# Turning softmax weights by 32x32 blocks on VectorE and moving the blocks by transfers, in a gated cross-attention and mixture kernel

## The chip, the cores and the metric

The kernel runs on one core of one Trainium2 chip. The metric is the time of one execution on the device, in microseconds (us). Before the change the median of three runs is 1311.29 us (1310.93 to 1311.45).

## The reference

There are 8 batches; x and the context are (8, 512, 2048) in float32. The last axis is cut into patches of 128 columns, and each patch attends within itself with 8 heads of 32 rows. Cut to what matters:

```python
def xattn(qk, v, masks, Wq, bq, Wk, bk, Wv, bv, Wo, bo):   # per patch of W = 128 columns
    q   = einsum('ed,bdw->bew', Wq, qp) + bq[:, None]       # 256 x 128
    k   = einsum('ed,bdw->bew', Wk, qp) + bk[:, None]
    val = einsum('ed,bdw->bew', Wv, vp) + bv[:, None]
    scores = einsum('bhdi,bhdj->bhij', qh, kh) / sqrt(32)
    scores = where(mp[:, :, None, :] > 0, scores, -1e9)
    attn = softmax(scores, axis=-1)
    o = gelu(einsum('bhij,bhdj->bhdi', attn, vh), approximate=False)
    return (einsum('de,bew->bdw', Wo, o) + bo[:, None]) * masks

x = x + tanh(g_xattn) * xattn(layernorm(x), ctx, mask, ...)
x = x + tanh(g_ffn) * ffn(layernorm(x), ...)   # router over 64 experts, the 8 best weights,
                                               # flat * their sum + weights @ expert_bias
```

## The kernel before

The columns of all batches are cut into 32 chunks of 512 (four per batch), and each chunk into two pairs of patches. The main loop (L816) handles one pair per turn, g from 0 to 61; such a turn is called a slot here. An even slot takes the first pair of chunk ch = g // 2, an odd one the second. Pairs 62 and 63 are handled by a written-out tail from L1025 on. The order of the work is written out by hand: every engine executes its instructions in the order in which the code issues them, and waits at an instruction until its operands are there.

A slot does, in TensorE's order: the scores of pair g (L412, 32 matmuls into four PSUM banks sc0 to sc3); the weighing of pair g - 2 (weigh, L487, tile pa); in even slots two row blocks of the output product of chunk ch - 2 (attend, L524, tile po), in odd slots the router's logits of chunk ch - 2 (L557, tile pl); then the queries and keys of the next chunk, in half of their rows (L343), by a seven-product scheme: seven blocks of two matmuls in four PSUM banks (tile qk). After that come the values of the next chunk (L391, tile pv), in even slots the turning of x (turn_x, L549, tile px), in odd slots two more blocks of the output product, and the mixture of experts of an older chunk (mixed, L695, tile pb).

The softmax of pair g: VectorE forms maxima over the keys from the scores and writes the negated scores to SBUF (maxima, L431, 16 instructions, 128x128 each); ScalarE takes the exponentials with their sums (exps, L446, 16 instructions); VectorE inverts the sums and POOL multiplies (divide, L458, once for each of the two patches). The weights then lie with the query on the partition, and the weighing needs the key there. They are turned one slot later, in pair g - 1's four steps of four TensorE transposes (turn, L468, tile pt), each copied out of PSUM by ScalarE (turned, L482, tile atT). In an even slot, two steps stand before the queries and keys, one among the values and one after turn_x; in an odd slot one before, two within (by the function between, L915) and one after the queries and keys.

Keys are multiplied by 1/sqrt(32) where the mask is on and by 0 where it is off (mask, L296, and L387). The same tile becomes an additive bias afterwards (mask_bias, L301) and is added in maxima. The eviction of the values adds bv on VectorE (L406). Gelu follows the weighing (L520), on ScalarE.

Buffers: the products qk, po, pl and pb share two PSUM buffers in turn (tag mm, function product at L311), except where a caller names one of the score banks: in the steady slots pv takes sc0, and an odd slot's two po take sc1 and sc2. Transposes and pa share two others (tag tr). A buffer's next product waits until the engine that reads the last one is done. The weights at have four buffers of one patch each.

SP issues nearly all DMAs, in program order: context (L102), normalized input (L96), x for the residual (L113), pieces of x for the statistics (L91, after the bn_stats of the piece before in that buffer), masks (L107) and the store (L711). The transfers use eight completion semaphores in turn.

In every eight slots, one batch of the mixture is prepared: an aggregate of statistics (fin 2), the choice of experts (fin 3, gather_halves, add_halves and choose), and the selection of the 8 best (fin 4, select and turn_weights, tile pw).

Of the kernel before, what the change touches and what calls it, by code (L numbers as in the profile page):

```python
# [15 lines left out]
P = 128  # L16
EPS = 1e-5
NEG = -1e9
# [4 lines left out]
def flamingo_gated_kernel(  # L23
# [43 lines left out]
    SW = 512  # L67
    scale = 1.0 / math.sqrt(DH)
# [54 lines left out]
    bv_sb = const.tile([P, DK], F32, name="bv_sb")  # L123
# [30 lines left out]
    def load_rest():  # L154
# [3 lines left out]
        nc.sync.dma_start(bv_sb, bv.partition_broadcast(P))  # L158
        with nc.allow_non_contiguous_dma(reason="short bias vectors onto partitions"):
            nc.sync.dma_start(bq_sb, bq.rearrange("(t p) -> p t", p=P))  # L160
            nc.sync.dma_start(bk_sb, bk.rearrange("(t p) -> p t", p=P))
            nc.sync.dma_start(bo_sb, bo.rearrange("(t p) -> p t", p=P))
        nc.sync.dma_start(gates[:, 0:1], g_xattn.partition_broadcast(P))
# [130 lines left out]
    qss, kss, vTs, m01s = {}, {}, {}, {}  # L294

    def mask(ch):  # L296

        m01s[ch] = work.tile([P, CW], F32, tag="m01", name=f"m01_{ch}")
        nc.vector.tensor_scalar(m01s[ch], mks[ch], 0.0, scale, ALU.is_gt, ALU.mult)

    def mask_bias(ch):  # L301

        nc.vector.tensor_scalar(m01s[ch], m01s[ch], 0.0, NEG, ALU.is_equal, ALU.mult)

# [15 lines left out]
    def first_queries_and_keys():  # L320
# [4 lines left out]
        for m in range(NM):  # L325
            for i, (w, e, pt) in enumerate(parts):
# [10 lines left out]
                else:  # L337
                    nc.vector.scalar_tensor_tensor(
                        kss[0][:, e, :], pt, bk_sb[:, e : e + 1], m01s[0], ALU.add, ALU.mult
# [3 lines left out]
    def queries_and_keys(ch, e, between):  # L343
# [6 lines left out]
        s1, s5, u2, u4 = (  # L350
            work.tile([P, CW // 2], F32, tag=t, name=f"{t}_{ch}_{e}", bufs=1)
            for t in ("s1", "s5", "u2", "u4")
        )
# [25 lines left out]
        u3 = work.tile([P, CW // 2], F32, tag="s1", name=f"u3_{ch}_{e}", bufs=1)  # L379
# [7 lines left out]
        nc.vector.tensor_tensor(k, k, m01s[ch], ALU.mult)  # L387
# [14 lines left out]
    def values_out(ch, h):  # L402
# [3 lines left out]
        nc.vector.tensor_tensor(vT, pv, bv_sb[:, None, :].to_broadcast([P, NPP, DK]), ALU.add)  # L406
# [5 lines left out]
    def scores(g):  # L412
# [14 lines left out]
        at = [work.tile([P, H, W], F32, tag="at", name=f"at_{g}_{i}", bufs=4) for i in range(NPP)]  # L427
# [3 lines left out]
    def maxima(g, qs):  # L431
# [4 lines left out]
        for q in qs:  # L436
            i = q // 2
            bias = m01s[ch][:, hf * HW + i * W : hf * HW + (i + 1) * W]
            for r in (2 * (q % 2), 2 * (q % 2) + 1):
                for e in range(NE):  # L440
                    nc.vector.tensor_tensor_reduce(  # L441
                        p["at"][i][:, e * HR + r, :], p["sc"][r][:, i, e, :], bias, -1.0, BIG,
# [25 lines left out]
    def turn(g, k):  # L468
# [3 lines left out]
        if e == 0:  # L472
            p["atT"][i] = work.tile([P, H, W], F32, tag="atT", name=f"atT_{g}_{i}")
# [5 lines left out]
    def copy(engine, out_, in_):  # L479
        (engine.tensor_copy if engine is nc.vector else engine.copy)(out_, in_)  # L480

    def turned(g, k, engine=nc.scalar):  # L482
        p = pairs[g]
        i, e = k // NE, k % NE
        copy(engine, p["atT"][i][:, e * HR : (e + 1) * HR, :], p.pop("pt"))

    def weigh(g):  # L487
# [7 lines left out]
        for i in range(NPP):  # L495
            for h in range(H):
                e, r = h // HR, h % HR
                nc.tensor.matmul(  # L498
                    pa[r * DH : (r + 1) * DH, e, i, :], vTs[ch, hf][:, i, h * DH : (h + 1) * DH],
                    p["atT"][i][:, h, :], start=True, stop=True,  # L500
# [19 lines left out]
    def gelu(ch, cs=whole):  # L520
        o = os_[ch][:, :, cs]
        nc.scalar.activation(o, o, AF.Gelu)  # L522
# [143 lines left out]
    def turn_weights(b, mps=range(NM // 2)):  # L666
        t = experts[b]
        rest, s = t["rest"], span(mps)
        if 0 in mps:

            pool, tag = (work, "s1") if late else (small, "wT")
# [98 lines left out]
    for m in range(NM):  # L770
# [6 lines left out]
        if m == NM - 1:  # L777
            mask(0)
            weight_sums()
            values_out(0, 0)  # L780
            values_out(0, 1)
            values_out(1, 0)
        next(projections)
    mask_bias(0)
# [31 lines left out]
    for g in range(NG - NH):  # L816
# [5 lines left out]
        g2 = g - 2 if g >= 2 else None  # L822
# [14 lines left out]

        def turn_(k):
            if g1 is not None:
                turn(g1, k)  # L840
                turned(g1, k)
# [18 lines left out]
        if g2 is not None:  # L860
            weigh(g2)
            weighed(g2)
# [11 lines left out]
        exps(g, 0)  # L874
        if even:
# [4 lines left out]
            exps(g, 1)  # L880
            exps(g, 2)
            if g > 0:
                mask(nxt)
            read_x(len(over), over)
            turn_(0)
            turn_(1)
            exps(g, 3)
            if fin != 4:
                for k in steps:
                    scale_x(mb, k)  # L890
            if g > 0:
                divide(g, 0)
            if g == 0:
                load_mask(2)
        else:
            exps(g, 1)
            if lch is not None:
                logits(lch)
                logits_out(lch)
            if g > 1:  # L900
                read_x(len(over), over)
            turn_(0)
            exps(g, 2)
            exps(g, 3)
            for k in steps:
                scale_x(mb, k)
            if g > 1:
                divide(g, 0)
# [5 lines left out]

        def between(i):  # L915
            if even:
                if g == 0 and i == 0:
                    divide(g, 0)
                    mask(nxt)
                turn_x_(i)  # L920
            elif i == 0:
                if g == 1:
                    divide(g, 0)
                turn_(1)
                if fin == 3:
                    gather_halves(b4)
                if pch is not None:
                    gelu(pch)
            else:
                if g == 1:  # L930
                    read_x(len(over), over)
                turn_(2)
                if pch is not None and nxt < last:
                    load_mask(nxt + 1)

# [3 lines left out]
        if not even:  # L939
            mask_bias(nxt)  # L940
# [3 lines left out]
        divide(g, 1)  # L944
        if not even and nxt < last:
# [3 lines left out]
            sums_of_x(nxt + 1, 0)  # L949
# [278 lines left out]
```

## Time and profile before

| what | value |
|---|---|
| median of 3 runs | 1311.29 us |
| span of the profiled execution, first to last instruction | 1309.1 us |
| busy: POOL | 796.3 us (61%) |
| granted TensorE clock, mean | 0.999 of full speed |
| an even slot (598.53 to 618.34) | 19.81 us: TensorE 19.81, VectorE 14.44, ScalarE 12.80, POOL 16.27 |
| an odd slot (618.34 to 638.22) | 19.88 us: TensorE 19.88, VectorE 12.92, ScalarE 13.63, POOL 7.86 |
| eight slots (378.91 to 538.31) | 159.40 us: TensorE 159.40, VectorE 114.22, ScalarE 108.08, POOL 100.18 |
| DMA | 173.40 MB, mean 132 GB/s; the SP queue 40.0% of 16 engines' span |

PE is TensorE's matmul, PEld its weight load, DVE VectorE, ACT ScalarE, SPq the issuing queue of SP. Busy times are of one profiled execution. Lines such as "L462 POOL ... xN | busy, mean | idle <- releaser" name a line of the kernel, the engine, the output and input tiles with buffer numbers left out, how many instructions there are, their busy time in us, the mean of one in ns, and how long the engine stood idle before them and for whom. In a timeline the columns are start and duration in us; the durations of neighbours overlap a little, so costs are taken from one start to the next. A matmul of float32 counts as two instructions.

### The profile page before, as it was taken

To read this page: it belongs to the slowest core of one execution; us is meant where nothing else is said; L and a number is where in the kernel's file an instruction comes from. 1 tells how busy PE (TensorE), PEld (TensorE's weight loads), DVE (VectorE), ACT (ScalarE), POOL (GpSimd) and SP (SyncE) were. 2 spreads that over 40 slices of the span, in tenths; PEclk is the share of its full clock that TensorE was granted. 3 is DMA by queue.
4 is the path that set the end of the run, shared out by engine and by line. 5 is a ranking of instruction groups with operands and counts; after the bars stand their busy time and mean duration, and the time that the engine had idled before them with its cause. 6 is when DMAs were issued, how large, how long until landed. Compare 5 with 4: busy or idle time off the path is not lost.

```text
span 1309.1 us, 27778 instructions
## 1 busy us (share of the span) xinstructions
PE 1292.1 (99%) x9532; PEld 941.1 (72%) x9532; DVE 923.7 (71%) x3605; ACT 872.2 (67%) x2843; POOL 796.3 (61%) x817
## 2 busy tenths in 40 slices
PE   8999999999999999999999999999999999999997
PEld 5777777777777777777777777777777777777653
DVE  5777676777677767777677776677776776666776
ACT  2776776676675766766676766677756767657654
POOL 3655456765566755566655666656666665566645
PEclk9999999999999999999999999999999999999999
DMA  8444324344345353444443453533543423423124
GB/s 273 111 126 122 112 78 137 106 161 127 116 153 162 123 167 97 136 165 142 140 148 95 154 169 124 159 108 123 165 151 132 159 63 127 138 97 106 69 78 177
DMA packets 109725, 173.40 MB, mean 132 GB/s; under 512 B 9232, under 2 KB 43664, under 8 KB 109456
## 3 DMA queue, kind: packets, MB, share of 16 engines
q1 hardware_dynamic: 107264, 168.75, 40.0%
q10 hardware_dynamic: 2320, 2.88, 0.6%
q8 instruction: 75, 1.23, 0.4%
q14 instruction: 66, 0.54, 0.1%
HBM read 138.06 MB, written 33.55 MB: 131 GB/s over the span
## 4 chain that ended last, share of the span: by engine, by line
PE 91%; ACT 3%; DVE 3%; DMA 1%; POOL 1%; issue 0%; DVEq 0%; ACTq 0%
PE qk L360 27%; PE po L528 17%; PE pv L397 15%; PE pt L476 8%; PE sc L422 5%; PE pa L498 5%; PE pb L702 5%; PE pl L563 4%; PE px L552 4%; ACT at L453 2%; DMA xr<-in_x 1%; DVE st L547 1%; DVE st L249 1%; PE pf L327 1%; ACT atT L480 0%
## 5 line engine op out<-in xcount | busy, mean ns | idle before, releaser
L462 POOL TENSOR_TENSOR at<-at,rsum 128x1024 f32<-128x1024 f32 x128 | 244.2, 1908 | 291.1 <-DVE rsum L461 269.2
L453 ACT ACTIVATE at<-at,nmx 128x128 f32<-128x128 f32 x1024 | 396.4, 392 | 3.2 <-DVE nmx L441 3.2
L397 PE MATMUL pv<-wv_sb,cx 128*128 128x256 f32 x1024 | 237.8, 380 | 1.7 <-DMA cx<-in_ctx 1.6
L528 PE MATMUL po<-o,wo_sb 128*128 128x512 f32 x512 | 234.1, 599 | 0.4 <-ACT o L522 0.4
L441 DVE CUSTOM_DVE_ANT_0 at<-sc,m 128x128 f32<-128x128 f32 x1024 | 220.7, 286 | 7.6 <-PE sc L422 7.4
L397 PEld LDWEIGHTS pv<-wv_sb,cx 128*128 128x128 f32 x1024 | 187.5, 191 | 24.8 <-DMA cx<-in_ctx 3.2
L537 POOL TENSOR_TENSOR xr<-t,xr 128x512 f32<-128x512 f32 x124 | 161.4, 1313 | 65.8 <-DVE t L534 65.7
L453 ACT ACTIVATION_READ_ACCUMULATOR at<-at,nmx 128x1 f32 x1024 | 194.9, 190 | 0.0
L480 ACT COPY o<-pa 128x512 f32<-128x512 f32 x63 | 36.9, 585 | 230.3 <-PE pa L498 230.3
L480 ACT COPY atT<-pt 128x512 f32<-128x512 f32 x254 | 140.5, 576 | 52.9 <-PE pt L476 52.7
L528 PEld LDWEIGHTS po<-o,wo_sb 128*128 128x128 f32 x512 | 94.3, 190 | 100.6 <-issue 83.9
L476 PEld LDWEIGHTS pt<-ident,at 128*128 128x128 f32 x1024 | 121.8, 141 | 57.2 <-issue 35.5
L476 PE MATMUL pt<-ident,at 128*128 128x128 f32 x1024 | 150.7, 275 | 1.3 <-ACT atT L480 0.9
L534 DVE SCALAR_TENSOR_TENSOR t<-po,bo_sb,mk 128x512 f32<-128x512 f32 x128 | 95.7, 749 | 62.5 <-PE po L528 62.2
L480 ACT COPY x1T<-px 128x512 f32<-128x512 f32 x120 | 70.2, 585 | 96.8 <-PE px L552 96.6
L360 PE MATMUL qk<-xt,wq_sb 128*128 128x256 f32 x496 | 128.0, 380 | 1.6 <-DVE u L368 1.6
L360 PE MATMUL qk<-xn,wk_sb 128*128 128x256 f32 x496 | 127.5, 380 | 0.0
L360 PE MATMUL qk<-xn,ws 128*128 128x256 f32 x496 | 127.3, 379 | 0.0
L360 PEld LDWEIGHTS qk<-xn,ws 128*128 128x128 f32 x496 | 94.2, 190 | 12.8
L720 DVE TENSOR_TENSOR xr<-pb,xr 128x512 f32<-128x512 f32 x122 | 78.2, 685 | 29.4 <-PE pb L702 29.4
L360 PEld LDWEIGHTS qk<-xn,wk_sb 128*128 128x128 f32 x496 | 89.4, 190 | 9.7
L422 PEld LDWEIGHTS sc<-ks,qs 32*128 32x128 f32 x2048 | 63.2, 186 | 45.3 <-DVE t L534 18.2
(123 smaller groups left out, 2077.7 us busy)
## 6 DMA issues: line engine op xcount, KB each, us to landing
out_dram<-xr SPq DMA_DIRECT2D x63, 512.0 KB, 3.5
cx<-in_ctx SPq DMA_DIRECT2D x61, 512.0 KB, 5.3
raw<-in_x SPq DMA_DIRECT2D x112, 256.0 KB, 3.4
xn<-in_x SPq DMA_DIRECT2D x28, 1024.0 KB, 7.8
xr<-in_x SPq DMA_DIRECT2D x28, 1024.0 KB, 7.6
mk<-in_mask_Bx1x_ff SPq DMA_DIRECT2D x32, 256.0 KB, 5.1
xr<-in_x SPq DMA_DIRECT2D x12, 256.0 KB, 6.9
cx<-in_ctx ACTq DMA_DIRECT2D x2, 512.0 KB, 8.2
```

The costliest lines, as they stand in the source:

```text
L360: nc.tensor.matmul(out_, w_[:, j, es], xb[:, j, :], start=(j == 0), stop=(j == NM // 2 - 1))
L397: nc.tensor.matmul(pv[:, i, :], cx[:, m, i * W : (i + 1) * W], wv_sb[:, m, :], start=(m == 0), stop=(m == NM - 1),)
L422: nc.tensor.matmul(sc[r][:, i, e, :], qss[ch][rows[r], e, ws], kss[ch][rows[r], e, ws], start=True, stop=True,)
L441: nc.vector.tensor_tensor_reduce(p["at"][i][:, e * HR + r, :], p["sc"][r][:, i, e, :], bias, -1.0, BIG, ALU.add, ALU.min, p["nmx"][:, r, i ...
L453: nc.scalar.activation(at, at, AF.Exp, bias=p["nmx"][:, r, i, e : e + 1], scale=-1.0, accum_out=p["rsum"][:, i, h : h + 1],)
L462: (engine or nc.gpsimd).tensor_tensor(p["at"][i], p["at"][i], rs[:, :, None].to_broadcast([P, H, W]), ALU.mult)
L476: nc.tensor.transpose(pt[:, r, :], p["at"][i][:, e * HR + r, :], ident)
L480: (engine.tensor_copy if engine is nc.vector else engine.copy)(out_, in_)
L528: nc.tensor.matmul(po[:, cs], wo_sb[:, e, m * P : (m + 1) * P], os_[ch][:, e, cs], start=(e == 0), stop=(e == NE - 1),)
L534: nc.vector.scalar_tensor_tensor(t[:, cs], po[:, cs], bo_sb[:, m : m + 1], mks[ch][:, cs], ALU.add, ALU.mult)
L537: (engine or nc.gpsimd).tensor_tensor(xc, t[:, cs], xc, ALU.add)
L720: nc.vector.tensor_tensor(xc, pt, xc, ALU.add)
```

## The change

1. In the slots, TensorE's turning (turn, turned) and its ScalarE copies are gone. VectorE turns each patch's weights in 32x32 squares, one instruction of 128x1024 per patch (turn_blocks), and then SP moves the squares between partitions with 16 transfers for a pair, each 32 partitions by 2 KB, from SBUF to SBUF (move_blocks). The tail still turns pairs 62 and 63 on TensorE.
2. Pair g - 1 is weighed in slot g (before: g - 2), and within the queries and keys, after the second PSUM bank. Its moving operand is read as four runs of 32 elements.
3. The keys aren't multiplied by the mask. The bias is made from the mask at once (NEG is -1e30), the maxima take the scale -1/sqrt(32), and mask_bias is gone.
4. The values are evicted by a plain copy on ScalarE; bv is added as the bias of gelu, which is split into its two row blocks.
5. Scratch tiles s1, u2, u3 and u4 of the queries and keys now lie in the result tiles themselves. The weights at have two buffers, blocks and atT one each.
6. Order: all exps stand before the bn_stats of leftover pieces and divide(g, 0); divide(g, 1) moves into the queries and keys; scale_x follows the moves; the sums of x are made together; norm stands ahead of the values' eviction.

```diff
-        m01s[ch] = work.tile([P, CW], F32, tag="m01", name=f"m01_{ch}")
-        nc.vector.tensor_scalar(m01s[ch], mks[ch], 0.0, scale, ALU.is_gt, ALU.mult)
-    def mask_bias(ch):
-        nc.vector.tensor_scalar(m01s[ch], m01s[ch], 0.0, NEG, ALU.is_equal, ALU.mult)
+        biases[ch] = work.tile([P, CW], F32, tag="bias", name=f"bias_{ch}")
+        nc.vector.tensor_scalar(biases[ch], mks[ch], 0.0, NEG, ALU.is_le, ALU.mult)
...
-        s1, s5, u2, u4 = (
-            work.tile([P, CW // 2], F32, tag=t, name=f"{t}_{ch}_{e}", bufs=1)
-            for t in ("s1", "s5", "u2", "u4")
-        )
+        s5 = work.tile([P, CW // 2], F32, tag="s5", name=f"s5_{ch}_{e}", bufs=1)
+        s1, u2, u3, u4 = k[:, c1], q[:, c2], q[:, c1], k[:, c2]
...
-        nc.vector.tensor_tensor(k, k, m01s[ch], ALU.mult)
...
-        nc.vector.tensor_tensor(vT, pv, bv_sb[:, None, :].to_broadcast([P, NPP, DK]), ALU.add)
+        copy(engine, vT, pv)
...
+    def turn_blocks(g, i):
+        p = pairs[g]
+        if i == 0:
+            p["blocks"] = work.tile([P, W // Q, NPP, H, Q], F32, tag="blocks", name=f"blocks_{g}", bufs=1)
+        nc.vector.transpose(
+            p["blocks"][:, :, i, :, :].rearrange("p b h j -> p h b j"),
+            p["at"][i].rearrange("p h (b j) -> p h b j", j=Q),
+        )
+    def move_blocks(g):
+        p = pairs[g]
+        t = p.pop("blocks")
+        w = work.tile([P, W // Q, NPP, H, Q], F32, tag="atT", name=f"atT_{g}", bufs=1)
+        for a in range(W // Q):
+            for b in range(W // Q):
+                nc.sync.dma_start(
+                    w[b * Q : (b + 1) * Q, a, :, :, :], t[a * Q : (a + 1) * Q, b, :, :, :]
+                )
+        for i in range(NPP):
+            p["atT"][i] = w[:, :, i, :, :].rearrange("p a h q -> p h a q")
...
-                    pa[r * DH : (r + 1) * DH, e, i, :], vTs[ch, hf][:, i, h * DH : (h + 1) * DH],
-                    p["atT"][i][:, h, :], start=True, stop=True,
+                    pa[r * DH : (r + 1) * DH, e, i, :].rearrange("p (a q) -> p a q", q=Q),
+                    vTs[ch, hf][:, i, h * DH : (h + 1) * DH],
+                    p["atT"][i][:, h, :, :], start=True, stop=True,
...
-        nc.scalar.activation(o, o, AF.Gelu)
+        for e in range(NE):
+            o = os_[ch][:, e, cs]
+            nc.scalar.activation(o, o, AF.Gelu, bias=bv_sb[:, e : e + 1])
...
         scores(g)
-        if g2 is not None:
-            weigh(g2)
-            weighed(g2)
         maxima(g, (0, 1))
...
         def between(i):
-            if even:
-                if g == 0 and i == 0:
-                    divide(g, 0)
-                    mask(nxt)
-                turn_x_(i)
-            elif i == 0:
-                if g == 1:
-                    divide(g, 0)
-                turn_(1)
+            if i == 0:
+                if g1 is not None:
+                    weigh(g1)
+                    weighed(g1)
+                if g == 0:
+                    mask(nxt)
+                divide(g, 1)
                 if fin == 3:
                     gather_halves(b4)
                 if pch is not None:
                     gelu(pch)
+                    table_of_exps()
             else:
+                turn_x_(0)
...
-                turn_(2)
                 if pch is not None and nxt < last:
                     load_mask(nxt + 1)
+                turn_blocks(g, 0)
...
         queries_and_keys(nxt, h, between)
-        if not even:
-            mask_bias(nxt)
+        turn_blocks(g, 1)
+        move_blocks(g)
+        if fin != 4:
+            for k in steps:
+                scale_x(mb, k)
```

## The prediction

> **What bounds the kernel now.** I read the engine totals first, then the chain that ended last, then the costliest groups, and last the timeline of two neighbouring slots, TensorE first and then VectorE.
>
> ```profile
> PE 1292.1 (99%) x9532; PEld 941.1 (72%) x9532; DVE 923.7 (71%) x3605; ACT 872.2 (67%) x2843; POOL 796.3 (61%) x817
> ...
> PE 91%; ACT 3%; DVE 3%; DMA 1%; POOL 1%; issue 0%; DVEq 0%; ACTq 0%
> PE qk L360 27%; PE po L528 17%; PE pv L397 15%; PE pt L476 8%; PE sc L422 5%; PE pa L498 5%; PE pb L702 5%; PE pl L563 4%; PE px L552 4%; ACT at L453 2%; DMA xr<-in_x 1%; DVE st L547 1%; DVE st L249 1%; PE pf L327 1%; ACT atT L480 0%
> ```
>
> TensorE is busy for 99% and makes 91% of the chain. The turning of the weights (pt, L476) is 8% of it, about 105 us. No other engine is over 71%. Groups:
>
> ```profile
> L462 POOL TENSOR_TENSOR at<-at,rsum 128x1024 f32<-128x1024 f32 x128 | 244.2, 1908 | 291.1 <-DVE rsum L461 269.2
> ...
> L441 DVE CUSTOM_DVE_ANT_0 at<-sc,m 128x128 f32<-128x128 f32 x1024 | 220.7, 286 | 7.6 <-PE sc L422 7.4
> ...
> cx<-in_ctx SPq DMA_DIRECT2D x61, 512.0 KB, 5.3
> raw<-in_x SPq DMA_DIRECT2D x112, 256.0 KB, 3.4
> xn<-in_x SPq DMA_DIRECT2D x28, 1024.0 KB, 7.8
> ```
>
> The timeline of TensorE in an even slot (scores at 598.53) shows where the turns stand; columns are start, duration, engine, line:
>
> ```profile
> 604.18 1.04 PE L476 MATMUL pt<-ident,at 128*128 128x128 f32 x8
> 605.06 1.03 PE L360 MATMUL qk<-xn,wk_sb 128*128 128x256 f32 x4
> ...
> 614.15 0.60 PE L476 MATMUL pt<-ident,at 128*128 128x128 f32 x4
> 614.58 1.89 PE L397 MATMUL pv<-wv_sb,cx 128*128 128x256 f32 x8
> ...
> 616.75 0.60 PE L476 MATMUL pt<-ident,at 128*128 128x128 f32 x4
> 617.28 1.13 PE L702 MATMUL pb<-eb_sb,wT 64*128 64x512 f32 x4
> 618.34 0.93 PE L422 MATMUL sc<-ks,qs 32*128 32x128 f32 x21
> ```
>
> From one start to the next, the turns take 0.88 + 0.43 + 0.53 = 1.84 us of the even slot's 19.81. In the odd slot (618.34 to 638.22, 19.88 us) the four gaps at 622.32, 626.27, 628.43 and 629.74 give 0.49 + 0.44 + 0.44 + 0.43 = 1.80. VectorE at the same places:
>
> ```profile
> 619.64 0.28 DVE L441 CUSTOM_DVE_ANT_0 at<-sc,m 128x128 f32<-128x128 f32 x1
> ...
> 623.02 0.69 DVE L581 TENSOR_TENSOR lgT<-pl,lgT 128x512 f32<-128x512 f32 x1
> ...
> 642.89 0.75 DVE L534 SCALAR_TENSOR_TENSOR t<-po,bo_sb,mk 128x512 f32<-128x512 f32 x1
> 644.07 0.75 DVE L534 SCALAR_TENSOR_TENSOR t<-po,bo_sb,mk 128x512 f32<-128x512 f32 x1 [0.43 <-PE po L528]
> ```
>
> In both slots VectorE is with the maxima until 4.67 us after the scores start (642.89 - 638.22; 623.02 - 618.34), and only then empties the first product. Today TensorE does pa and pt meanwhile.
>
> **Part 1, TensorE loses the turns.** 62 of 64 pairs lose four turns. An even slot becomes 19.81 - 1.84 = 17.97 us, an odd one 19.88 - 1.80 = 18.08.
>
> **Part 2, what is late next.** pa moves from behind the scores to behind two bank pairs of the query product. So nothing stands between po (or pl) and that product, which uses the same two PSUM buffers in turn. Even slot: po is through at 1.10 + 3.54 = 4.64 us after the scores start, but the first bank waits until t of m=2 has emptied its buffer: 4.67 + 0.67 (604.38 to the next VectorE start at 605.05) + 0.07 for the signal = 5.41. TensorE stands 0.77. Odd slot: the second bank is wanted at 1.10 + 1.87 + 1.73 = 4.70 and waits for lgT: 4.68 + 0.69 + 0.07 = 5.44, so 0.74. Slots become 18.74 and 18.82, a pair of slots 37.56 against 39.69: 2.13 saved, not 3.64.
>
> **Part 3, VectorE.** It loses the key mask product (L387, 0.60 us start to start), the values' eviction (L406, 0.60) and in odd slots L303 (0.43). It gains two block transposes of 128x1024 per slot. No row shows one. Bounds: L303 does 512 elements of one source in 0.34 start to start, so twice that less its fixed part is about 0.61; POOL's pass over the same tile is 1.91. Nearest is bn_stats, one source, 512 elements in 0.60 (2.34 us for four at L547): 1024 at that slope, 0.53 more, is 1.13, which I take.
> Even slot in order: third bank pair through at 11.61 (5.41 + 1.73 + 1.73 + 1.01 + 1.73), u and ks until 12.61, transpose to 13.74, qs to 14.08, transpose to 15.21, four bn_stats to 17.55, two to 18.75. Then the adds of pb, which TensorE releases at 18.84. VectorE is just in time: cover 0.1 us. Each 0.1 us more per transpose costs 0.2 in each of 31 even slots, 6 us in all. Odd slots have over 1 us free (transposes end at 13.5, t is due at 16.2).
> The first transpose waits for POOL's divide. In even slots POOL has two xr adds (2.6) from 5.41, so the divides end at 9.9 and 12.6, before 12.61 and 14.08. qs now overwrites u in place and waits for POOL's L381, 13.3: also before it is due. Behind a waiting transpose would stand qs, bn_stats and the next maxima.
>
> **Part 4, the moves.** 16 transfers per pair, 32 partitions x 2 KB (64 KB), all on SP, which now issues 992 more. In the changed kernel's instruction order the transfers use eight completion semaphores in turn, and each waits for the one eight before it, so the ninth move waits for the first to land. An issue takes 0.38 to 0.46 us in the SP rows; I take 0.42. Landing of 64 KB has no row: from 256 KB (3.4) and 1 MB (7.6) a straight line gives 2.35; bounds are 0, and 5.3 as for 512 KB, which is what eight in flight carry. Even slot: 15.21 + 15 x 0.42 + 2.35 = 23.9, that is 5.1 in the odd slot, where pa is due at 5.44 + 1.73 = 7.17. Room 2.0 us. From odd to even it is 13.5 to a due time of 18.82 + 8.88, room 5. Hidden, then.
> SP's queue behind them: raw (2), the store, cx, then the 1 MB xn. The odd slot's moves leave SP at 20.2, so xn is issued at about 22.0, lands 7.8 later at 11 in the even slot; norm on ScalarE starts at 14.2. Covered by 3 us.
> Here a page speaks against the change: the Trainium skill, "DMA: Bandwidth & Descriptors", Rules for kernel authors, says to coalesce small transfers, since under 64 KB mostly overhead is paid, and its bandwidth table has 64 KB at 0.95 us. Run one after another, 16 would take 15.2 us by that, past the due time by some 5 us each odd slot, an estimate of +150 us. The rows decide otherwise here, because SP need not wait for one before it issues the next.
>
> **Part 5, pa's operand.** It reads four runs of 32 elements in place of 128 in a row. No row shows such a moving operand; from 0 to a doubling of its 1.01 us per slot. I take 0: L360's matmuls take 380 ns each whether their operand is a slice of xn or all of a row of xt.
>
> **Part 6, edits at nothing.** The eviction of values goes to ScalarE behind norm: done by 17.9, due at the next scores (18.74); cover 0.8, and uncovered it would cost up to its own 0.58 per slot. The copies of atT leave ScalarE (140 us). Gelu in two halves is 0.2 us more, while pv runs on TensorE. The bias is one pass as the mask was.
>
> **The sum.** Slots 8 to 61 are 27 pairs: -57.5. Slots 4 to 7 have no pb: about -5. In each of 7 batches, select (2.65 us) stands between the transposes and pw (+0.8) and the aggregate (0.62) falls in the full even slot (+0.5): +9. Slots 0 to 3 are 10 to 18 us long, and there pa waits for moves that land 8.7 us after the transposes: +6. The two last pairs still turn on TensorE; slot 62 loses pair 61's turns: -1.5. Total -49. The profiled span of 1309.1 becomes 1260; the median of 1311.29 is 2.2 over that span, so 1262.
>
> **Rivals.**
> (a) The moves come late: slower. If a move lands in 5.3 us like cx, the ninth is issued at 5.3, the sixteenth at 8.2, and the last lands 13.5 after the transposes, 2.8 past the 10.7 us there are. 31 odd slots: +87, 1349. It decides from a landing of 3.9 us (2 x 3.9 + 7 x 0.42 = 10.7). For: it lies between the rows of 256 KB and 512 KB, and only 32 partitions are at each end. Against: 64 KB is a quarter of the smaller one.
> (b) The transpose costs 1.91: VectorE bounds the even slots, 2 x 0.78 x 31 = +48, 1310: no change.
> (c) pa doubles: 62 x 1.01 = +63, 1325. Against: nothing else in the trace slows with a slice.
> (d) The waits of part 2 don't come, since t and lgT could fall earlier: 58 slots x 0.75 = -44, 1218. Against: 4.67 is measured in both slots.
>
> **Chances.** Forecast 0.50 (1240 to 1285), (d) 0.10, (b) 0.12, (a) 0.21, (c) 0.07. Faster by over 0.2%, about what a measurement here can tell from no change: 0.50 + 0.10 + half of (b) + 0.04 of (a) = 0.70. Within: 0.03 of (b) and 0.01 of (a) = 0.04. Slower: 0.16 + 0.07 + 0.03 = 0.26. The range takes in (d), (b), (c) and the milder half of (a): 1215 to 1335.
>
> **What would show it.** In the profile after: PE pt down to some 32 transposes; a wait of the query product for t and lgT of about 0.75 us per slot; transposes near 1.13; pa with hardly a wait for DMA. Wrong if pa waits long for atT (rival a), if maxima start over 1.5 us after the scores' start (rival b), or if pa lasts over 1.1 us (rival c).

## The result, and the profile after

| | median | spread | ratio to before, 95% interval |
|---|---|---|---|
| before | 1311.36 us | 1310.93 to 1311.45 | |
| after | 1389.72 us | 1381.01 to 1392.31 | 1.0586 [1.0554, 1.0617] |

The change makes the kernel 78 us slower. The forecast was 1262 us, in a range from 1215 to 1335. The profiled execution of after took 1388.15 us, its span is 1386.3 us, and the mean granted TensorE clock in it is 0.970 of full speed (before 0.999).

The page of after, engine totals, the granted clock over the span, the main queue and the chain:

```profile
PE 1249.2 (90%) x8540; PEld 853.9 (62%) x8540; DVE 995.4 (72%) x3574; ACT 794.4 (57%) x2688; POOL 791.8 (57%) x817
...
PEclk9879999999999999999999999999999999999999
...
q1 hardware_dynamic: 155008, 233.70, 56.6%
...
PE 31%; DVE 25%; DMA 19%; SPq 11%; issue 5%; ACT 4%; POOL 4%; DVEq 0%; POOLq 0%; ACTq 0%
PE qk L355 11%; SPq L503 10%; DVE at L441 9%; DMA xn<-in_x 7%; PE po L552 7%; PE pv L390 5%; DMA out_dram<-xr 3%; DMA xr<-in_x 3%; DVE blocks L491 3%; PE pa L520 3%; DVE t L558 2%; DMA atT<-blocks 2%; PE sc L418 2%; DVE lg L650 2%; PE pb L7
```

TensorE lost 992 of its 9532 matmuls (16 transposes in each of 62 pairs), as was meant. But its busy time fell by 43 us only, while the span grew by 77 us: it is busy for 90% now, it stands for 31% of the chain in place of 91%, and most of the rest is VectorE, transfers and SP's issuing (SPq, L503: the moves). The clock row has an 8 and a 7 near the start, where before has nines.

What TensorE waited for in after (total, times, longest):

```profile
PE pa L520 <- DMA atT<-blocks: 39.5, 18, 10.6
PE sc L418 <- ACT vT L396: 38.6, 25, 7.5
PE qk L355 <- DVE t L558: 16.1, 24, 1.1
...
PE qk L355 <- DVE lgT L605: 7.2, 18, 0.7
PE qk L355 <- DVE lgT L603: 4.0, 8, 0.5
```

The last three are the waits that part 2 of the forecast worked out. The first two were not in its sum: the weighing waits for the moved weights, and the scores wait for the values, which ScalarE evicts late. SP's timeline in after (start, duration, line) shows why:

```profile
608.59 10.01 SPq L503 DMA_DIRECT2D atT<-blocks  x16
618.70 1.02 SPq L92 DMA_DIRECT2D raw<-in_x  x2
...
620.82 1.45 SPq L97 DMA_DIRECT2D xn<-in_x  x1
...
632.74 10.03 SPq L503 DMA_DIRECT2D atT<-blocks  x16
```

Sixteen moves take SP 10.0 us of issuing, 0.63 us each. That is not time spent waiting for the move eight before: among all that SP waited for ahead of its 992 moves, the landings of earlier transfers have 6.3 us in all, one of them a move's, and nearly all the rest is VectorE's turn:

```profile
SPq L503 <- DVE blocks L491: 319.5, 61, 10.8
...
SPq L503 <- DMA atT<-blocks: 0.6, 1, 0.6
```

Everything behind them on the queue starts when the sixteenth is out: raw at 618.70 and xn at 620.82 here. The landing is not the trouble; the page's rows have 64 KB moves landing in the time that the forecast took (2.35), and xn later than before (9.0 against 7.8):

```profile
atT<-blocks SPq DMA_DIRECT2D x992, 64.0 KB, 2.0
...
xn<-in_x SPq DMA_DIRECT2D x28, 1024.0 KB, 9.0
```

To place the loss, I measured each slot in the trace from its first scores to the next slot's. The four columns on the right are means in us over slots 12 to 60, by the slot's number modulo eight (3 chooses the experts, 4 selects them).

| run | median, us | slots 0-7 | slots 8-61 | even slots (0, 2 of 8) | odd slots (1, 7 of 8) | slot 3 of 8 | slot 4 of 8 |
|---|---|---|---|---|---|---|---|
| before | 1311.4 | 130.8 | 1069.5 | 19.81 | 19.88 | 20.31 | 20.03 |
| after | 1389.7 | 173.2 | 1101.1 | 19.96 | 19.94 | 22.38 | 21.47 |
| one transfer (e1) | 1309.4 | 134.4 | 1065.3 | 19.26 | 19.16 | 21.71 | 21.25 |
| one transfer, sums late (e9) | 1291.9 | 133.8 | 1045.9 | 19.26 | 19.16 | 19.73 | 20.44 |
| one transfer, sums late, t early (e14) | 1250.2 | 133.2 | 1006.3 | 18.26 | 18.37 | 18.78 | 19.53 |
| all turned on TensorE (e3) | 1409.6 | 140.5 | 1159.0 | 22.09 | 20.91 | 21.30 | 22.34 |
| mended, all late (e13) | 1274.7 | 139.2 | 1015.1 | 18.56 | 18.51 | 19.45 | 19.35 |

Of after's loss, 42 us lie in the first eight slots and 32 in the 54 that follow. The columns leave out slots 5 and 6 of eight. Slot 5 is like the other odd ones; slot 6 is longer than the slots 0 and 2: 20.75 us in after, 19.93 in e1 and e9 and 20.30 in e14, where before has 19.81. The largest single wait is in slot 1 (TensorE's timeline, the bracket is idle time and what ended it):

```profile
45.64 1.03 PE L355 MATMUL qk<-xn,ws 128*128 128x256 f32 x4
57.30 1.94 PE L520 MATMUL pa<-atT,vT 128*32 128x128 f32 x32 [10.63 <-DMA atT<-blocks]
59.16 2.08 PE L355 MATMUL qk<-xt,wq_sb 128*128 128x256 f32 x4
...
61.94 1.03 PE L355 MATMUL qk<-xt,wq_sb 128*128 128x256 f32 x4
```

The moves of pair 0 are issued from 45.56 on for 10.09 us, in a slot that took 13.5 us before. After 10.63 us of idling the same 32 matmuls of pa take 1.94 us in place of 1.08, and qk 2.08 in place of 1.03: the clock is at half. The windows say so too (length, busy time of PE, PEld, DVE, ACT, POOL, granted clock, DMA share, GB/s):

```profile
57.30:61.00 3.70, 3.70 (x36) 2.99 (x37) 0.00 (x0) 0.58 (x1) 0.00 (x0) 0.50 0.38 130
```

### The profile page after: what moved, and what is told of

It is laid out like the page before. It is cut to its first block, busy times and chain, and to the rows that moved or that the text cites. A ratio compares the mean times of both kernels' runs of the same rounds, so it can differ in the third digit from the quotient of the medians.

```text
span 1386.3 us, 27197 instructions
## 1 busy us (share of the span) xinstructions
PE 1249.2 (90%) x8540; PEld 853.9 (62%) x8540; DVE 995.4 (72%) x3574; ACT 794.4 (57%) x2688; POOL 791.8 (57%) x817
## 4 chain that ended last, share of the span: by engine, by line
PE 31%; DVE 25%; DMA 19%; SPq 11%; issue 5%; ACT 4%; POOL 4%; DVEq 0%; POOLq 0%; ACTq 0%
PE qk L355 11%; SPq L503 10%; DVE at L441 9%; DMA xn<-in_x 7%; PE po L552 7%; PE pv L390 5%; DMA out_dram<-xr 3%; DMA xr<-in_x 3%; DVE blocks L491 3%; PE pa L520 3%; DVE t L558 2%; DMA atT<-blocks 2%; PE sc L418 2%; DVE lg L650 2%; PE pb L726 2%
## 5 line engine op out<-in xcount | busy, mean ns | idle before, releaser
L441 DVE CUSTOM_DVE_ANT_0 at<-sc,bias 128x128 f32<-128x128 f32 x1024 | 220.9, 286 | 29.2 <-PE sc L418 29.2
L552 PE MATMUL po<-o,wo_sb 128*128 128x512 f32 x512 | 241.2, 614 | 0.0
L355 PE MATMUL qk<-xn,wk_sb 128*128 128x256 f32 x496 | 136.3, 397 | 27.3 <-DVE t L558 16.1
L491 DVE STREAM_TRANSPOSE blocks<-at 128x1024 f32<-128x1024 f32 x124 | 152.7, 1231 | 0.0
L355 PE MATMUL qk<-xt,wq_sb 128*128 128x256 f32 x496 | 138.5, 403 | 7.6 <-DVE qs L363 7.6
L374 DVE SCALAR_TENSOR_TENSOR qs<-qk,bq_sb,qs 128x256 f32<-128x256 f32 x62 | 30.0, 483 | 158.9 <-PE qk L355 158.9
L418 PEld LDWEIGHTS sc<-ks,qs 32*128 32x128 f32 x2048 | 70.4, 194 | 88.9 <-ACT vT L396 59.0
L418 PE MATMUL sc<-ks,qs 32*128 32x128 f32 x2048 | 85.8, 293 | 40.7 <-ACT vT L396 38.6
L520 PE MATMUL pa<-atT,vT 128*32 128x128 f32 x2048 | 72.6, 284 | 43.2 <-DMA atT<-blocks 39.5
L355 PEld LDWEIGHTS qk<-xt,wq_sb 128*128 128x128 f32 x496 | 90.4, 197 | 28.7 <-DVE qs L363 7.8
```

The costliest lines, as they stand in the source:

```text
L355: nc.tensor.matmul(out_, w_[:, j, es], xb[:, j, :], start=(j == 0), stop=(j == NM // 2 - 1))
L418: nc.tensor.matmul(sc[r][:, i, e, :], qss[ch][rows[r], e, ws], kss[ch][rows[r], e, ws], start=True, stop=True,)
L441: nc.vector.tensor_tensor_reduce(p["at"][i][:, e * HR + r, :], p["sc"][r][:, i, e, :], bias, -scale, BIG, ALU.add, ALU.min, p["nmx"][:, r, ...
L491: nc.vector.transpose(p["blocks"][:, :, i, :, :].rearrange("p b h j -> p h b j"), p["at"][i].rearrange("p h (b j) -> p h b j", j=Q),)
L520: nc.tensor.matmul(pa[r * DH : (r + 1) * DH, e, i, :].rearrange("p (a q) -> p a q", q=Q), vTs[ch, hf][:, i, h * DH : (h + 1) * DH], p["atT ...
L552: nc.tensor.matmul(po[:, cs], wo_sb[:, e, m * P : (m + 1) * P], os_[ch][:, e, cs], start=(e == 0), stop=(e == NE - 1),)
```

## The experiments

The experiments are numbered e1 to e15, and those that answer one question stand together. My theory after the traces: the loss is the issuing of the moves on SP (10.0 us per pair), which makes the weighing late and pushes xn behind it; a smaller part is the choice of experts, which now runs beside GpSimd's sums; and waits of a few us also cost TensorE its clock. The rivals: the moved bytes themselves, the block turns on VectorE, or the change's other edits.

### e1, e2 and e15: the same bytes in one transfer, in four, and in sixteen

```diff
-        for a in range(W // Q):
-            for b in range(W // Q):
-                nc.sync.dma_start(w[b * Q : (b + 1) * Q, a, :, :, :], t[a * Q : (a + 1) * Q, b, :, :, :])
+        nc.sync.dma_start(w, t)
```

e2 has four transfers, of t[rows] to w[rows] for the four groups of 32 partitions. e15 keeps all sixteen, and only their target changes: w[a * Q : (a + 1) * Q, b, :, :, :].

> The 16 moves of a pair become one transfer of the same 1 MB, written back to its own partitions, so the blocks aren't moved between partitions and the output is not the reference's; everything else stays. Theory (SP's issue pace: 16 issues at 0.63 us are 10.0 us per pair, pa and xn wait for their end): one issue of about 0.6 us is left, pa's wait on the moved blocks (39.5 us of the span on TensorE) and ScalarE's on xn (34.9 us) go, and the time falls to 1285 to 1325 us. Rival (bytes: the 65 MB more on the queue and their landing slow every other load): stays at 1370 us or above. Rival (transposes and the other edits cost it): 1350 us or above with the waits on the blocks gone.

> The 16 moves become four transfers of 256 KB, each within its own 32 partitions, so the blocks aren't moved between partitions and the output is not the reference's. Theory (cost per issue): four issues take about 2.5 us instead of 10.0, near the single transfer's time, 1290 to 1335 us. Rival (cost by bytes): as with one transfer and with sixteen, 1370 us or above. If a transfer's issue costs in proportion to its size, four take as long as sixteen and nothing is gained.

> The 16 moves stay sixteen transfers of 64 KB, but each goes from 32 partitions to the same 32 partitions, so the blocks aren't moved between partitions and the output is not the reference's. Theory (the cost is SP's issuing of sixteen transfers): as after, 1375 to 1395 us, with 10 us of issuing per pair. Rival (the crossing between partitions is what costs, and the single transfer was quick because it left that out): 1335 us or below.

Measured: 1309.44 us with one, ratio 0.9985 [0.9976, 0.9994]; 1322.60 us with four, 1.0085 [1.0070, 1.0100]. With sixteen in place it is 1388.63 us, 1.0597 [1.0577, 1.0618], the time of after. The bytes are innocent: 238 MB are moved in all of these kernels. So is the crossing of partitions, which e15 leaves out. The 80 us are gone with 15 of the 16 issues. Issuing from a second queue, which would have told SP's time apart from the number of transfers, was not run; the 10.0 us of SP against landings of 2.0 us speak for SP. With one and with four, TensorE's wait for the moved weights falls from 39.5 to 5.1 and 9.5 us, and ScalarE's for xn from 34.9 to nothing and 4.7. Four issues took 3.27 us, not 2.5: one is 0.82 us for 256 KB, 0.63 for 64 KB, and 0.47 for 1 MB over all 128 partitions, so neither their number nor their size alone sets it.

Where the issues strike can be read from TensorE's waits in slots 8 to 61, of after and then of e1:

```profile
PE sc L418 <- ACT vT L396: 30.2, 22, 2.1
...
PE pa L520 <- DMA atT<-blocks: 12.8, 13, 1.8
```

```profile
PE sc L418 <- ACT vT L396: 13.7, 9, 1.9
```

In e1 the wait for the moves is absent there. So of the 36 us between the two in these slots, 12.8 are the moves and 16.5 the values, which are evicted behind norm, which waits for xn (in e5, where xn comes early, this wait is 13.8 us, as in e1). In slots 0 to 7, 20.1 of 39 us are the moves (25.2 against 5.1).

But 1309 is not 1262 either: with the moves all but free the change is worth 2 us. Slots 3 and 4 of every eight are still long, slot 6 is no shorter than before, and the others have lost 0.55 and 0.72 us instead of 1.07.

### e3 and e10: all weights turned on TensorE again

```diff
-        turn_blocks(g, 1)
-        move_blocks(g)
+        turn_here(0, 1)
...
                 values_out(c_, h_)
+            turn_here(2, 3)
```

In e10, weigh(g1) and weighed(g1) also stand right behind scores(g).

> The change's other edits stay (mask product gone, values' evictions on ScalarE, sums of x together, pairs weighed a slot sooner), but the weights are turned on TensorE in each slot as before, with no block turns on VectorE and no moves. Theory (the moves carry most of the loss, the sums beside the choice of experts some 2 us in each of 13 slots): 1315 to 1345 us. Rival (the side edits are harmless and the moves carry all): 1305 to 1315 us. Rival (the loss lies in the side edits): 1360 us or above.

> As the kernel that turns all weights on TensorE (1409.6 us), but the pair before is weighed right behind the scores, where the product's 1.0 us stands in front of the po or pl product, instead of between queries and keys. Theory (the moved product exposed TensorE's wait for t of 0.75 us and for lgT of 0.53 us, and broke the row of query products, about 0.1 us at each break): 1.0 us less in even and 0.7 us less in odd slots, 27 pairs, 1355 to 1370 us. Rival (where the product stands doesn't matter, turning in the same slot costs it all): 1400 us or above.

Measured: 1409.63 us, 1.0748 [1.0732, 1.0764], and 1350.33 us, 1.0299 [1.0284, 1.0314]. I had expected e3 between 1315 and 1345; it came where the rival that put the loss in the side edits had it (1360 or above), and that miss was the most useful one. e10 came out 5 us below its range. Without any moves the kernel is slower than after itself. Taken against e1, it says that turning on VectorE is worth 100 us when the moves cost nothing (the forecast's part 1 has 62 pairs by 1.82, 113 us), though e3's turns stand in other places than before's. And it says that the rest of the change, with the turning put into the pair's own slot, costs 98 us against before. e10 shows where 59 of these are: in the place of pa. Behind the scores pa fills the time in which TensorE waits for t or lgT; between the banks it leaves that wait open and breaks the row of query products. This is e1's timeline in an even slot whose scores start at 639.94:

```profile
645.49 1.13 PE L355 MATMUL qk<-xn,wk_sb 128*128 128x256 f32 x4 [0.75 <-DVE t L554]
646.46 1.03 PE L355 MATMUL qk<-xt,ws 128*128 128x256 f32 x4
647.32 1.03 PE L355 MATMUL qk<-xn,wk_sb 128*128 128x256 f32 x4
648.18 1.03 PE L355 MATMUL qk<-xn,ws 128*128 128x256 f32 x4
649.14 1.08 PE L516 MATMUL pa<-atT,vT 128*32 128x128 f32 x32
650.15 1.13 PE L355 MATMUL qk<-xt,wq_sb 128*128 128x256 f32 x4
651.12 1.03 PE L355 MATMUL qk<-xn,ws 128*128 128x256 f32 x4
```

The wait is nearly the forecast's: 0.75 us of idle time by the profile, but 0.91 from start to start, as the forecast counted its 0.77 (645.49 - 641.04, less 3.54 for po); the first product stands 5.55 after the scores against 5.41. What was missing are the breaks: from start to start a row of four products takes 0.86 to 0.87 us within the run, and 0.96 or 0.97 behind the wait, ahead of pa and behind pa. The other 39 us of e10 lie in the even slots (20.84 against 19.81 in before, some 28 us) and in the first eight (139.7 against 130.8); their cause is open.

### e4 to e8: one wait at a time

e4 puts the weighing behind all queries and keys:

```diff
-                if g1 is not None:
-                    weigh(g1)
-                    weighed(g1)
...
         queries_and_keys(nxt, h, between)
+        if g1 is not None:
+            weigh(g1)
+            weighed(g1)
```

> The product of the moved weights and their evictions stand behind all queries and keys of the even slot instead of between them, some 4 us later; nothing else changes. Theory: TensorE's wait for the last move (39.5 us in all, 1 to 2 us per pair and more in the first slots) is covered by the second half of queries and keys; xn is still late behind the moves, so part of it is given back: 1350 to 1378 us. Rival (xn behind the moves sets the pace of the even slot, the wait at pa only takes its place): 1383 to 1393 us.

Measured: 1346.12 us, 1.0268 [1.0251, 1.0285], 44 us less than after and a little better than the theory's range. The wait for the moves falls from 39.5 to 3.8 us; the one of the scores for vT is still 23.9. The edit moves the weighing, and ScalarE's eviction of it, in odd slots as in even ones. Slots 8 to 61 come to 1066.7 us, which is e1's 1065.3: there the later weighing wins back all that the issues cost. What is left of it lies in slots 0 to 7 (164.7 against 134.4).

e5 issues xn ahead of the moves:

```diff
-            if nxt < last and nxt + 1 >= NCH:
-                load_xn(nxt + 1)
...
         queries_and_keys(nxt, h, between)
+        if not even and nxt + 1 < last and nxt + 2 >= NCH:
+            load_xn(nxt + 2)
```

> xn of the pair after next is issued in the odd slot ahead of the 16 moves instead of in the even slot behind them; nothing else changes. Theory: ScalarE's wait on xn (34.9 us in all) goes, norm, the values' evictions and the scores come sooner in the even slots, while pa still waits for the moves, which are now issued up to 1.5 us later: 1365 to 1383 us. Rival (pa's wait alone sets the pace): 1385 to 1400 us.

Measured: 1375.81 us, 1.0491 [1.0475, 1.0507]. ScalarE's wait for xn is gone, the even slots come to e1's 19.26, and odd slots grow, since pa's wait rises from 39.5 to 51.5 us: 14 us are left of it, as the theory said.

e6 moves two of the three sums of x back to the slot's end in the slots that choose the experts:

```diff
-            for k in range(3):
+            for k in range(1 if fin == 3 else 3):
                 sums_of_x(nxt + 1, k)
...
+            if fin == 3 and nxt < last:
+                for k in (1, 2):
+                    sums_of_x(nxt + 1, k)
```

> In the slots that choose the experts (every eighth, 13.60 us into the choice VectorE's operations take 974 ns instead of 281) two of the three sums of x go back from beside the choice to the slot's end; nothing else changes. Theory (VectorE's small operations beside GpSimd's sums are slow, the choice lands late, ScalarE's values and the scores after it): the slot's 22.38 us fall by 1 to 2 us, 8 such slots, and the time by 6 to 18 us, to 1370 to 1382 us. Rival (the choice is hidden, the slot is long for the late xn): 1386 to 1392 us.

Measured: 1372.14 us, 1.0457 [1.0438, 1.0475], 17.6 us less; slot 3 falls from 22.38 to 20.47. VectorE's rows of the choice, of after and then of e6:

```profile
L650 DVE SCALAR_TENSOR_TENSOR lg<-lg,rs,rb_sb 128x64 f32<-128x64 f32 x28 | 25.6, 974 | 0.2
```

```profile
L650 DVE SCALAR_TENSOR_TENSOR lg<-lg,rs,rb_sb 128x64 f32<-128x64 f32 x28 | 6.1, 280 | 0.2
```

The same 28 instructions take 974 ns beside GpSimd's two-input sums (1.27 to 1.32 us each) and 280 ns without them (281 in before). In after four of them last from 609.45 to 613.26; ScalarE's exps of the choice wait for them for 5.70 us, the values are evicted behind those, and the scores wait. TensorE's timeline of after:

```profile
615.70 1.73 PE L418 MATMUL sc<-ks,qs 32*128 32x128 f32 x32 [1.90 <-ACT vT L396]
617.36 5.40 PE L552 MATMUL po<-o,wo_sb 128*128 128x512 f32 x8
```

The wait is 1.90 us, and the product after it, at a clock of 0.71 in the window from 615.70 to 620.00, takes 5.40 us where it took 3.70 in before: nearly the wait once more. The Trainium skill, "SBUF — State Buffer", SBUF: two separate sides, says that VectorE with two SBUF inputs and GpSimd share a pair of ports by a lock that one of them holds for the whole instruction; the 974 ns against 280 agree with that, with one sum after another running on GpSimd in those 3.81 us.

e7 turns the weights of slots 0 to 7 on TensorE (as e3 does, for g < 8), and e8 joins the edits of e4 to e7.

> Slots 0 to 7 turn their weights on TensorE, all later ones by block turns and moves. Theory (in the first slots the moves share SP with the input loads, TensorE idles up to 10 us and its clock falls; slots 0 to 7 together are 42 us longer than before): 30 to 42 us are given back, 1346 to 1360 us. Rival (the first slots are slow for another reason, the earlier weighing or the sums): 1378 us or above.

> The last four edits together: weights of slots 0 to 7 turned on TensorE, weighing behind the queries and keys, xn ahead of the moves, two sums of x at the end of the slots that choose. Theory: with the waits for the moves covered, TensorE's fewer turns are at last worth something in slots 8 to 61: 1270 to 1310 us, no slower than before. Rival (the evictions and VectorE's turns are the next bound, the even slots stay near 20 us): 1315 to 1340 us.

Measured: 1352.48 us, 1.0313 [1.0272, 1.0353], and 1312.94 us, 1.0012 [1.0003, 1.0022]. Slots 0 to 7 fall from 173.2 to 140.5 in e7, which is nearly all of its gain. e8 lies between its two ranges: the waits for the moves are gone (2.4 us), slots 8 to 61 are 20 us shorter than before, and the first eight 18 us longer. e7, which turns as e3 does there, has 10 of these 18; which of the other edits costs the remaining 9 was not separated.

### e9 and e14: what the change could give without the issues

e9 joins e1 and e6. e14 adds that VectorE empties the first product between the two halves of the maxima:

```diff
         maxima(g, (0, 1))
+        if even and xch is not None:
+            attend(xch, 2)
+        elif not even and lch is not None:
+            logits(lch)
+            logits_out(lch)
         maxima(g, (2, 3))
```

> The one transfer of 1 MB per pair (blocks not moved between partitions, so not the reference's output) together with two sums of x back at the end of the slots that choose; nothing else changes against the single transfer's kernel (1309.4 us). There slots 3 and 4 of every eight are 21.71 and 21.25 us against 19.16 and 19.26 of their kind, 4.5 us per batch of eight. Theory (GpSimd's sums slow VectorE's choice, the scores wait 1.9 us for the values, and TensorE's clock is halved for some 2 us after that wait): both come near their kind, 7 batches give back 20 to 32 us, 1278 to 1290 us. Rival (the choice itself, or the moves' bytes, make these slots long): 1302 us or above.

> One transfer of 1 MB per pair (blocks not moved between partitions, so not the reference's output), two sums of x at the end of the slots that choose, and t or the logits' sum between the halves of the maxima: the change without the 16 issues, without the slow choice and without the wait for t or lgT. Theory: against 1291.9 us 0.5 to 0.75 us less in each of 54 slots, 1250 to 1265 us, which is what the forecast hoped for. Rival (VectorE's turns bound the slots): 1280 us or above.

Measured: 1291.91 us, 0.9849 [0.9834, 0.9863], and 1250.16 us, 0.9532 [0.9518, 0.9547]. e9 is just above its range: slot 3 came to 19.73, slot 4 only to 20.44. e14 removes the waits for t and lgT and 42 us with them (forecast for rival d: 44). VectorE's block turns hold up no ordinary slot at 18.3 us. Slot 6 of eight is the exception, 20.30 us: in the slot ahead of it six bn_stats stand behind the turns, VectorE empties that slot's po late, and the next scores, which need its banks, wait. VectorE's and then TensorE's timeline of e14 (scores from 424.80):

```profile
425.32 1.39 DVE L554 SCALAR_TENSOR_TENSOR t<-po,bo_sb,mk 128x512 f32<-128x512 f32 x2
```

```profile
424.80 0.48 PE L418 MATMUL sc<-ks,qs 32*128 32x128 f32 x2
426.11 0.48 PE L418 MATMUL sc<-ks,qs 32*128 32x128 f32 x2 [0.83 <-DVE t L554]
426.77 1.16 PE L418 MATMUL sc<-ks,qs 32*128 32x128 f32 x28 [0.17 <-DVE t L554]
```

### e11, e12 and e13: versions with real moves

e11 has e5's and e6's edits, turns pairs 0 to 7 on TensorE a slot later, as before does, and weighs behind the queries and keys in odd slots only. e12 adds e14's edit. e13 weighs late in even slots too:

```diff
-                if not old and even:
-                    weigh(g1)
-                    weighed(g1)
...
-        if not old and not even:
+        if not old:
             weigh(g1)
             weighed(g1)
```

> A version meant to beat both: slots 0 to 7 turn on TensorE a slot later as the kernel before does (130.8 us for these slots there, 149.2 in the run with all four edits), later odd slots weigh behind all queries and keys and even ones between them (where the moves are in time and the even slot was 19.26 instead of 19.55), xn goes ahead of the moves, two sums of x go to the end of the slots that choose. Theory: 14 us less in slots 0 to 7 and 8 us less in the even slots than the run with all four edits (1312.9): 1283 to 1300 us. Rival (the early slots or the choice hold it): 1305 us or above.

> The mended version, with VectorE emptying the first po product (even slots) or the logits' product (odd slots) between the two halves of the maxima instead of behind them. Theory (in every slot TensorE waits 0.75 or 0.53 us for t or lgT, because VectorE is with the maxima until 4.7 us after the scores start): these waits go, 27 pairs of 1.3 us at most, 1252 to 1275 us. Rival (VectorE's work in a slot is the pace, and the wait comes back at the next row of products): within 8 us of the mended version.

> The mended version with t early, and the weighing behind all queries and keys in the even slots too. Theory (once t comes early, even slots reach the product sooner than the moves land, TensorE's wait for them there is 32.8 us in all, and its clock falls after such a wait): the wait goes and the even slots of 20.0 us come to 18.6 to 19.3, 1268 to 1284 us. Rival (the even slots are bound by VectorE or by xn and only change the name of their wait): 1290 to 1298 us.

Measured: 1302.13 us, 0.9934 [0.9917, 0.9950]; 1295.33 us, 0.9875 [0.9860, 0.9889]; 1274.74 us (1268.03 to 1280.11), 0.9734 [0.9713, 0.9756]. e11 missed its range by 2 us; its slot 7, where the one way of turning gives over to the other, is 25.0 us long. e12 gave the rival's number for another reason. This is its longest wait, and then e13's:

```profile
PE pa L520 <- DMA atT<-blocks: 32.8, 19, 3.2
```

```profile
PE pa L520 <- DMA atT<-blocks: 6.7, 6, 2.1
```

With t early the even slots reached pa before the moves had landed; the wait had moved, not gone. Placed later in e13, pa waits for 6.7 us in all, and the kernel beats both before (by 2.7%) and after. It is 25 us from e14, whose moves are not issued sixteen times.

## Why the prediction was wrong

The step that failed is part 4, **"an issue takes 0.38 to 0.46 us in the SP rows; I take 0.42"**, and with it "Hidden, then". Fifteen issues were to take 6.3 us; sixteen took 10.0. The rows I had read were loads from and stores to memory; no row showed a transfer from SBUF to SBUF over 32 partitions, and I gave the landing two bounds and the issue none. Nor did those rows end at 0.46. SP's timeline of before has, in the even slot that the forecast worked from:

```profile
600.95 1.77 SPq L96 DMA_DIRECT2D xn<-in_x  x1
```

The room in the odd slot was 2.0 us, and 15 times 0.21 more is 3.2. Its second victim is the cover of 3 us for xn, which stood behind the moves on the same queue: in after one xn is issued 5.1 us after its slot's scores (620.82 - 615.70; forecast 3.2), though these came 1.90 late, and xn lands in 9.0 us at the median, not 7.8. The moves were not hidden, and neither was xn.

Point by point:

- **Part 1** (TensorE loses the turns, 113 us): right. An even slot of e1 can be built from it: 19.81 less 1.84 for the turns, 0.91 more for the wait and about 0.3 for three breaks is 19.2, and 19.26 is measured. e3 against e1 gives 100, with the turns in other places.
- **Part 2** (waits of 0.77 and 0.74): right in mechanism; from start to start they are 0.91 for t and 0.70 for lgT (in e1's odd slot 664.70 - 663.14, less 0.86; idle by the profile 0.75 and 0.53). Too small by the breaks of the row of products, about 0.1 us each, which were priced at nothing: e1's slots are 19.26 and 19.16 against 18.74 and 18.82. 27 pairs by 0.86 are 23 us, of which the longer wait for t is 4.
- **Part 3** (transpose 1.13): right. A turn is 1231 ns long and takes 1.15 us from start to start (605.82 to 606.97 in after). "VectorE is just in time" held in the ordinary even slots. "Odd slots have over 1 us free" failed in the one ahead of slot 6 of eight, where t was late (e14's rows above).
- **Part 4**, landing 2.35: right, 2.0 measured; rival (a) put the danger in the landing, and its threshold of 3.9 us was never reached. The late moves came by the issues. Rival (a) had the sign of it by another cause, and that after without the loss in the early slots comes near its 1349 is chance: it put 87 us on 31 odd slots, where the issues cost 36 in slots 8 to 61. "Covered by 3 us" for xn failed for the same reason: ScalarE waited 34.9 us for it.
- **Part 5** (pa's operand free): right, 1.02 us per slot at full clock (626.13 to 627.15 in after).
- **Part 6** (values' eviction behind norm, cover 0.8): the cover was xn being in time and the choice being quick. Both failed, and the scores waited 38.6 us for vT; with both mended in e9 it is 1.9.
- **The sum's "+9" for batches** left out the sums of x beside the choice: 17.5 us (e1 against e9, e6 against after). The order of GpSimd's work had been read for the divides and not for these.
- **The sum's "+6" for slots 0 to 3** assumed 8.7 us from the last transpose to the last landing; with 12 us, and with a half clock after long waits and loads queued behind the moves, slots 0 to 7 together are 42 us longer, 39 of them by the sixteen issues (against e1).

In numbers: forecast -49; breaks in TensorE's rows and the later t +23 (from slot lengths); the choice +17.5 (e1 against e9); the sixteen issues in place of one +80 (after against e1; e15 shows that it is these). That is +72 of the +78 measured. The remaining 7 us are not taken apart. Some 4 of them, an estimate, are slot 6 of eight: 0.67 us over the other even slots in e9, six times. Of the 80 us, the slots of after and e1 put 39 into slots 0 to 7 and 36 into slots 8 to 61. In slots 8 to 61 two waits make up 29.3 of the 36 (12.8 for the moves, 16.5 more for the values). How much of the rest is clock was not separated by a run of its own; the mean granted clock (0.970 against 0.988) allows at most 0.03 of 1386 us, 42 us, in after and 16 in e1.

## What to carry to other kernels

When work goes from an engine to transfers, price the issues on the queue as an engine's work of its own, with both bounds, and list what stands behind them on that queue; here one landing was 2.0 us, but sixteen issues were 10.0. Placing the consumer later (e4) won back 44 of the 80 us that the issues cost. A product that seems free to move may be what fills another product's wait: see what stands in its old place afterwards. An edit that shifts the order on GpSimd has to be read against what VectorE does at that moment.

## What the runs showed of the hardware that was not expected

- SP issues an SBUF to SBUF transfer of 32 partitions in 0.63 us (64 KB) or 0.82 us (256 KB), one of 128 partitions and 1 MB in 0.47 us, and loads of raw behind them take 1.1 us each in e2 in place of 0.5. The Trainium skill, "DMA: Bandwidth & Descriptors", Issuing engines are not separate DMA queues, says that the time to initiate a transfer is usually small relative to the transfer; here it is a third of one landing, and five landings for a pair.
- TensorE's granted clock fell to half not only after 10.63 us of idling but also after a wait of 1.90 us (0.71 as the mean of the 4.3 us that follow, 0.50 from 617.60 to 620.80), though not after each such wait: behind one of 1.90 us that ends at 719.36 in e1 it stayed at 1.00. The Trainium skill, "TensorE: Matmul & The Clock Gate", Part 1, names an idle window of about 3.4 us; the wait measured here is shorter.
- One VectorE instruction of 128x64 elements went from 280 to 974 ns beside GpSimd's sums.
